# Keys and values of a narrow attention projected ahead, its maxima through single PSUM banks, and a first attention that holds V stationary

## The chip, the cores and the metric

The kernel runs on one NeuronCore of a Trainium2 chip. The metric is the device time of one execution in microseconds (us), lower is better. Nine executions of the kernel before had a median of 1678.9 us (1672.92 to 1681.6). Engines are called by their names: TensorE (PE in the profile), VectorE (DVE), ScalarE (ACT), GpSimd (POOL) and SyncE (SP), which issues most transfers.

## The reference

A network of twelve blocks, each added to a residual `x` of shape [4, 128, 128] (batch, token, channel); most read a layernorm of it. Four blocks attend to a context of shape [4, 2048, 96]. Two of these are changed here, and a feed-forward block lies between two changes.

The first block (`_L0_xattn_ref`, the kernel's `bit_attention`) uses linear layers with ternary weights and int8-rounded activations. Its attention runs twice, and its keys, which are also its values, are 64 wide and used twice over:

```python
for Wa, ba in ((W_att0, b_att0), (W_att1, b_att1)):
    kv = bitnet_linear(image_embeds, Wa, ba)
    k = jnp.concatenate([kv, kv], axis=-1)
    scores = jnp.einsum('bse,bpe->bsp', fused, k) * inv_sqrt_e
    attn = jax.nn.softmax(scores, axis=-1)
    fused = fused + 0.1 * jnp.einsum('bsp,bpe->bse', attn, k)
```

The tenth block (`_L3_xattn_ref`, `narrow_attention`) has eight heads of sixteen channels:

```python
q = x @ Wq + bq
k = y @ Wk + bk          # y: the context
v = y @ Wv + bv
# heads of 16
weight = softmax(einsum('bhqd,bhkd->bhqk', q, k) * scale)
out = einsum('bhqk,bhkd->bhqd', weight, v) ... @ Wo + bo
```

The ninth (`_L2_ffn_ref`, `bit_ffn`) is layernorm, a quantized linear layer to 512, Gelu, layernorm, and a quantized linear layer back to 128.

## The kernel before

`Net` holds one method per block; they are called in order, and each passes `nxt()` to load the next block's weights. A framework allots tiles from pools (a pool of `bufs=n` reuses n buffers per tag and makes the next user wait for the last reader), and the order of instructions on each engine is fixed when the kernel is built. PSUM has eight banks of 512 float32 per partition.

**`bit_attention`** (L812 on) works in eight units: two rounds (`att0`, `att1`) times four batches. A unit's 2048 context positions are sixteen chunks of 128, in two groups g of eight. `scores(g)` (L959) writes transposed scores, 128 positions by 128 queries per chunk, with keys of even chunks in partitions 0 to 63 and those of odd chunks in 64 to 127. `reduce_max` (L961), a transpose (L966), a second reduction (L968) and a spreading transpose (L971) give the maximum; `weights(g)` subtracts it (L977) and takes the exponential (L979) into `p`. `values` (L988) holds each chunk of `p` stationary and streams 65 columns of `v`, 64 values and a column of ones that gives the softmax sum; then a reciprocal (L992), a scaling (L994), a transpose (L996) and an addition (L997) into `fused`. The loop interleaves units: maximum of i, scores 0 of i+1, weights of i, values of i-1, scores 1 of i+1, queries of i+2. At i = 3 and 4 a context mask is loaded and converted on GpSimd (L1027).

**`bit_ffn`** (L1768 on) needs the mean of its weights' absolute values: a matmul `tot` (L1786), then `wm`, `wi` and, per half, `t` twice and `qw` (L1788 to L1797), all on VectorE. `q_tr` transposes the quantized input, `h_ps` (L1828) is the first product. The second layernorm writes a tile `hn`.

**`narrow_attention`** (L593 on) keeps heads in groups of four, g = 0 to 3, each in 32 partitions; s = 0, 1 picks the group of four. After the layernorm and `q_ps`, `project(0)` computes keys `k_ps` (L645) and values `v_ps` (L656) of batch 0; `maxima(0, 0)` streams the keys past each head's queries (`s_ps`, L673), reduces them (L678), transposes the maxima (`m_tr`, L684) and adds them into spare rows of `q` (L685), so that the later scores come out already reduced by them. The loop then runs over batches b and halves s; `weighted` makes four steps of four chunks each: transposed scores `t_ps` (L697), their exponential `p` (L703), and, one step late, the values `av` (L710), whose seventeenth row is the softmax sum. Beside each step run one quarter of the next half's maxima and, while s and b allow, one piece of `project(b + 1)`. `finish` (copies of `av`, `o_tr`, `on_tr`, `y`) closes a batch after the first step of the next. PSUM: three double banks shared by `q_ps`, `k_ps`, `v_ps`, `s_ps` and `t_ps`, one bank for all small transposes, one for `av`. Copies out of PSUM alternate between ScalarE (L323) and VectorE (L325).

Of the kernel before, what the change touches and what calls it, by code (L numbers as in the profile page):

```python
# [19 lines left out]
B = 4  # L20
# [250 lines left out]
class Net:  # L271
# [320 lines left out]

    def narrow_attention(self, nxt):  # L593
# [7 lines left out]
        wqo, wkv = self.load("qo3"), self.load("kv3")  # L601
        scale = 1.0 / math.sqrt(ND)
        with ExitStack() as es:
# [3 lines left out]
            ps = es.enter_context(tc.tile_pool(name="na_sc", bufs=3, space=PSUM))  # L607
            mi = es.enter_context(tc.tile_pool(name="na_mi", bufs=1, space=PSUM))
# [4 lines left out]
            tr = mi.tile([P, B, P], F32, tag="mi", name="tr_x")  # L613
# [24 lines left out]
            def project(b):  # L638

                kT = wk.tile([P, 2, S], F32, tag="kT", name="kT")  # L640
                v = wk.tile([P, NCH, NH * VW], F32, tag="v", name="v")
                for at in range(0, S, 512):
                    mm = ps.tile([P, 2, 512], F32, tag="sc", name="k_ps")
                    for s in range(2):
                        nc.tensor.matmul(  # L645
                            mm[:, s], wkv[:, s * P : s * P + P],
                            self.ctxT[: DC + 1, b * S + at : b * S + at + 512], start=True, stop=True)
                    self.copy(kT[:, :, at : at + 512], mm)
                    yield kT, v
                for c in range(0, NCH, 6):  # L650
                    mm = ps.tile([P, 2, 512], F32, tag="sc", name="v_ps")
                    n = min(6, NCH - c)
                    for j in range(n):
                        at = b * S + (c + j) * P
                        w = NH * VW
                        nc.tensor.matmul(  # L656
                            mm[:, j // 3, j % 3 * w : j % 3 * w + w], self.ctxT[: DC + 1, at : at + P],
                            wkv[:, 2 * P : 2 * P + w], start=True, stop=True)
                    for j in range(0, n, 3):
                        k = min(3, n - j)  # L660
                        self.copy(
                            v[:, c + j : c + j + k].rearrange("p c w -> p (c w)"), mm[:, j // 3, : k * w])
                    yield kT, v

            def maxima(b, s, kT):

                qs = q[:, s, b * T : b * T + T]
# [1302 lines left out]
```

## Time and profile before

| | us |
|---|---|
| median of nine executions | 1678.9 |
| the profiled execution, its own time | 1678.22 |
| its span in the trace | 1676.2 |
| mean granted TensorE clock | 0.812 |
| TensorE busy (share of the span) | 1251.0 (75%) |
| VectorE busy | 999.3 (60%) |
| ScalarE busy | 620.6 (37%) |
| GpSimd busy | 140.8 (8%) |
| `bit_attention`, loop over units | 80.5 to 187.3 |
| `bit_ffn`, from the end of alibi to its `x` | 1302.5 to 1359.9 |
| `narrow_attention`, `q_ps` to first `t_ps` | 1367.3 to 1395.7 |
| `narrow_attention`, loop | 1395.7 to 1607.7 |

A line of the groups reads: line, engine, operation, output <- inputs, shape, count | busy us, mean ns of one | idle time of the engine before it and what ended that. An fp32 matmul appears as two records. The granted clock is a share of full speed, 1.00 or 0.50 at any moment. Starts are us from the start of the span.

### The profile page before, as it was taken

How to read it: one execution, taken by the hardware profiler on the slowest of the kernel's cores; microseconds unless marked ns; L12 is line 12 of the kernel's file. 1: busy time of each engine (PE TensorE's matmuls, PEld its weight loads, DVE VectorE, ACT ScalarE, POOL GpSimd, SP SyncE). 2: the span in 40 equal slices, each digit the busy share in tenths (PEclk: the TensorE clock that was granted, in tenths of full speed). 3: DMA queues.
4: the chain of work that ended last, by engine and by line, in shares of the span. 5: the costliest groups of instructions: out<-in, count | busy, mean ns of one | idle time of the engine just before them, and what ended most of it. 6: DMA issues, size and time to landing. Idle time of an engine off the chain costs nothing.

```text
span 1676.2 us, 15539 instructions
## 1 busy us (share of the span) xinstructions
PE 1251.0 (75%) x6142; PEld 675.5 (40%) x6142; DVE 999.3 (60%) x1568; ACT 620.6 (37%) x796; POOL 140.8 (8%) x108
## 2 busy tenths in 40 slices
PE   2689547677899999999847054989958148989857
PEld 0378412223434444444313032654426034555544
DVE  8955468994256676767567954124657665354335
ACT  3722255552145555646433001324523102333332
POOL 0010004462000000000001000000020100000000
PEclk9965558798579999999968576978978567898778
DMA  5000000005000000000010004000000000000010
GB/s 156 1 1 1 0 0 1 25 0 142 17 26 1 0 1 1 0 0 1 1 50 1 0 0 125 1 23 19 1 2 1 9 0 1 2 2 1 6 48 7
DMA packets 9371, 28.19 MB, mean 17 GB/s; under 512 B 1175, under 2 KB 7104, under 8 KB 8142
## 3 DMA queue, kind: packets, MB, share of 16 engines
q1 hardware_dynamic: 8174, 24.88, 5.1%
q10 hardware_dynamic: 1120, 2.27, 0.4%
q8 instruction: 50, 0.82, 0.2%
q14 instruction: 27, 0.22, 0.0%
HBM read 26.88 MB, written 0.26 MB: 16 GB/s over the span
## 4 chain that ended last, share of the span: by engine, by line
PE 63%; DVE 24%; ACT 5%; issue 4%; POOL 3%; DMA 1%; POOLq 0%; ACTq 0%; DVEq 0%; SPq 0%
PE sc L495 12%; PE av L529 12%; PE s_ps L673 4%; DVE na_m L678 3%; PE av L988 3%; PE mm L1317 3%; PE t_ps L697 3%; PE q_ps L438 2%; DVE h L1234 2%; PE av L710 2%; PE h_ps L1666 2%; PE y_ps L1673 2%; PE st L959 2%; PE y_ps L1239 2%; POOL hc L1237 1%
## 5 line engine op out<-in xcount | busy, mean ns | idle before, releaser
L495 PE MATMUL sc<-q_aug,ctxT 99*128 99x512 f32 x448 | 213.2, 602 | 1.8 <-DVE q_aug L439 1.8
L529 PE MATMUL av<-s,ctx 128*97 128x512 f32 x448 | 206.8, 597 | 6.6 <-ACT s L527 6.0
L526 DVE TENSOR_TENSOR s<-s,mbs 128x1024 f32<-128x1024 f32 x112 | 132.3, 1217 | 38.8 <-ACT mbs L521 38.8
L497 ACT COPY s<-sc 128x1024 f32<-128x1024 f32 x112 | 112.9, 1008 | 114.8 <-PE sc L495 114.8
L678 DVE TENSOR_REDUCE na_m<-s_ps 128x2 f32<-128x1024 f32 x64 | 75.8, 1220 | 91.2 <-PE s_ps L673 91.0
L527 ACT ACTIVATE s<-s 128x1024 f32<-128x1024 f32 x112 | 115.5, 1056 | 35.9 <-DVE s L526 35.3
L505 DVE TENSOR_TENSOR m<-m,s 128x1024 f32<-128x1024 f32 x72 | 87.9, 1220 | 66.3 <-ACT s L497 66.3
L529 PEld LDWEIGHTS av<-s,ctx 128*97 128x97 f32 x448 | 73.1, 165 | 125.0 <-issue 105.5
L495 PEld LDWEIGHTS sc<-q_aug,ctxT 99*128 99x128 f32 x448 | 82.7, 193 | 93.9 <-issue 82.7
L1239 PE MATMUL y_ps<-hc,consts 128*128 128x512 f32 x128 | 75.2, 722 | 33.7 <-POOL hc L1237 30.8
L703 ACT ACTIVATE p<-t_ps 128x1024 f32<-128x1024 f32 x64 | 62.0, 1021 | 92.4 <-PE t_ps L697 92.4
L1237 POOL TENSOR_TENSOR hc<-h,cs 128x1024 f32<-128x1024 f32 x32 | 77.5, 2430 | 86.2 <-DVE h L1234 86.0
L1234 DVE TENSOR_TENSOR_SCAN h<-dA,dbu 128x512 f32<-128x512 f32 x64 | 74.4, 1202 | 3.7 <-ACT dA L1231 3.5
L673 PE MATMUL s_ps<-kT,q 32*128 32x512 f32 x256 | 66.1, 720 | 1.9 <-ACT p L703 1.0
L341 POOL TENSOR_TENSOR ln_sq<-ln_xc 128x512 f32<-128x512 f32 (+1 forms) x19 | 23.3, 1226 | 507.0 <-DVE ln_xc L339 500.5
L697 PE MATMUL t_ps<-q,kT 32*128 32x128 f32 x1024 | 56.3, 329 | 8.8 <-DVE na_m L678 5.8
L1239 PEld LDWEIGHTS y_ps<-hc,consts 128*128 128x128 f32 x128 | 26.0, 222 | 83.2 <-POOL hc L1237 57.0
L697 PEld LDWEIGHTS t_ps<-q,kT 32*128 32x128 f32 x1024 | 46.6, 223 | 27.1 <-DVE na_m L678 14.7
L1231 ACT ACTIVATE dA<-delta,A 128x508 f32<-128x508 f32 x64 | 42.7, 688 | 33.1 <-DVE h L1234 32.2
L358 PE MATMUL tr_xnT<-consts,xn 128*128 128x128 f32 x32 | 8.8, 429 | 60.1 <-DVE xn L348 41.3
L988 PEld LDWEIGHTS av<-kv,p 128*128 128x128 f32 x256 | 53.2, 319 | 0.2 <-issue 0.2
L988 PE MATMUL av<-kv,p 128*128 128x65 f32 x256 | 52.9, 399 | 0.0
(574 smaller groups left out, 2083.6 us busy)
## 6 DMA issues: line engine op xcount, KB each, us to landing
w_moe<-in_moe SPq DMA_DIRECT2D x2, 2048.0 KB, 8.0
ctxT<-in_ctxT SPq DMA_DIRECT2D x4, 768.0 KB, 12.6
rows<-in_rows ACTq DMA_DIRECT2D x1, 2048.0 KB, 12.0
w_l3f<-in_l3f SPq DMA_DIRECT2D x1, 1920.0 KB, 8.0
w_l0f<-in_l0f SPq DMA_DIRECT2D x1, 1024.0 KB, 4.9
w_mamba<-in_mamba SPq DMA_DIRECT2D x1, 976.0 KB, 18.9
w_r<-in_r SPq DMA_DIRECT2D x1, 960.0 KB
consts<-in_consts SPq DMA_DIRECT2D x1, 832.0 KB, 17.2
```

The source lines that it names most:

```text
L495: nc.tensor.matmul(sc[:, i], self.ctxT[:, at : at + P], u.q, start=True, stop=True)
L497: nc.scalar.copy(s, sc)
L526: nc.vector.tensor_sub(p, p, bc_mid(u.mb, 2))
L527: nc.scalar.activation(p, p, AF.Exp)
L529: nc.tensor.matmul(u.av[: DC + 1], self.ctx[:, u.b * NCH + chunks[2 * j + i]], p[:, i], start=j + i == 0, stop=j == n - 1 and i == 1)
L673: nc.tensor.matmul(ts[g // 2][:, g % 2], qs[lo : lo + 32], kT[lo : lo + 32, s, j * 512 : j * 512 + 512], start=True, stop=True)
L678: nc.vector.tensor_reduce(part[:, at : at + 2], t, axis=AX, op=ALU.max, negate=True)
L697: nc.tensor.matmul(ts[g // 2][:, g % 2, j], kT[g * 32 : g * 32 + 32, s, at : at + P], qs[g * 32 : g * 32 + 32], start=True, stop=True)
L988: nc.tensor.matmul(av[:, 0:65], u.ts[g][:, h * (HC // 2) + c], u.v[:, ch], start=g + h + c == 0, stop=g + h == 2 and c == HC // 2 - 1)
L1234: nc.vector.tensor_tensor_scan(h[:, half], self.flat(dA), dbu[:, half], 0.0, ALU.mult, ALU.add)
L1237: nc.gpsimd.tensor_mul(hc, h, bc_mid(cs, 2))
L1239: nc.tensor.matmul(y[:, half], self.ident, hc[:, half], start=n == 0, stop=n == 15)
```

## The change

Three things are changed.

`narrow_keys`, new, is called after `alibi_attention`, ahead of `bit_ffn`. It loads the weights `kv3` (before, they came with the block's other weights) and projects keys and values of batches 0 and 1 through three single PSUM banks, every copy on ScalarE. Batches 2 and 3 are projected inside the loop of `narrow_attention`, in the s = 0 steps of b = 1 and 2, four pieces a step; a piece is now one bank.

In `narrow_attention` the double banks go from three to two and serve `t_ps` and `q_ps` only. A ring `sp` of three single banks serves `s_ps`, all small transposes and the projections. `maxima` handles one head per tile and reduces it by itself (128x512, where it was 128x1024); two heads are issued ahead of `t_ps` and two ahead of `av` in each step. `weighted` yields twice a step, and `finish` comes after the values of the first step.

In `bit_attention` V is stationary (64 columns) and `p` streams (128 columns). Even chunks write the output's partitions 0 to 63, odd ones 64 to 127. The softmax sums come from three additions on GpSimd per group and two matmuls with a matrix of ones, which leave the sum in every partition; its reciprocal (128x128) and a multiplication scale the values, a matmul with `fold` adds both halves into both, and one VectorE operation adds the result into `fused`. The column of ones and the transpose are gone.

In `bit_ffn` the second layernorm works in place and one tile takes another's buffer.

```diff
--- before.py
+++ after.py
@@ -590,6 +590,44 @@
 
 
 
+    def narrow_keys(self, es):
+        pool = es.enter_context(self.tc.tile_pool(name="na_w", bufs=1))
+        self.wkv = pool.tile(list(self.A["kv3"].shape), F32, name="w_kv3")
+        self.nc.sync.dma_start(self.wkv, self.A["kv3"])
+        self.kvp = es.enter_context(self.tc.tile_pool(name="na_kv", bufs=2))
+        self.kv = {}
+        with self.tc.tile_pool(name="na_kvps", bufs=3, space=PSUM) as ps:
+            for b in range(2):
+                for self.kv[b] in self.project(ps, b, self.nc.scalar.copy):
+                    pass
+
+    def project(self, ps, b, copy):
+
+        nc, wkv = self.nc, self.wkv
+        kT = self.kvp.tile([P, 2, S], F32, tag="kT", name="kT")
+        v = self.kvp.tile([P, NCH, NH * VW], F32, tag="v", name="v")
+        for at in range(0, S, 512):
+            for s in range(2):
+                mm = ps.tile([P, 512], F32, tag="s", name="k_ps")
+                nc.tensor.matmul(
+                    mm, wkv[:, s * P : s * P + P], self.ctxT[: DC + 1, b * S + at : b * S + at + 512],
+                    start=True, stop=True)
+                copy(kT[:, s, at : at + 512], mm)
+                yield kT, v
+        w = NH * VW
+        for c in range(0, NCH, 3):
+            mm = ps.tile([P, 512], F32, tag="s", name="v_ps")
+            n = min(3, NCH - c)
+            for j in range(n):
+                at = b * S + (c + j) * P
+                nc.tensor.matmul(
+                    mm[:, j * w : j * w + w], self.ctxT[: DC + 1, at : at + P],
+                    wkv[:, 2 * P : 2 * P + w], start=True, stop=True)
+            copy(v[:, c : c + n].rearrange("p c w -> p (c w)"), mm[:, : n * w])
+            yield kT, v
+
     def narrow_attention(self, nxt):
 
 
@@ -598,19 +636,19 @@
 
 
         nc, tc = self.nc, self.tc
-        wqo, wkv = self.load("qo3"), self.load("kv3")
+        wqo = self.load("qo3")
         scale = 1.0 / math.sqrt(ND)
         with ExitStack() as es:
             one = es.enter_context(tc.tile_pool(name="na1", bufs=1))
             wk = es.enter_context(tc.tile_pool(name="na2", bufs=2))
             pp = es.enter_context(tc.tile_pool(name="na3", bufs=4))
-            ps = es.enter_context(tc.tile_pool(name="na_sc", bufs=3, space=PSUM))
-            mi = es.enter_context(tc.tile_pool(name="na_mi", bufs=1, space=PSUM))
+            ps = es.enter_context(tc.tile_pool(name="na_sc", bufs=2, space=PSUM))
+            sp = es.enter_context(tc.tile_pool(name="na_s", bufs=3, space=PSUM))
             avp = es.enter_context(tc.tile_pool(name="na_av", bufs=1, space=PSUM))
             xn = one.tile([P, B, C], F32, name="xn")
             self.layernorm(one, self.x, xn)
             nc.vector.tensor_add(self.x, self.x, bc_mid(self.row("bo3"), B))
-            tr = mi.tile([P, B, P], F32, tag="mi", name="tr_x")
+            tr = sp.tile([P, B, P], F32, tag="s", name="tr_x")
             for b in range(B):
                 nc.tensor.transpose(tr[:, b], xn[:, b], self.ident)
             xT = one.tile([P, N], F32, name="xT")
@@ -635,52 +673,23 @@
                 os.append(t)
             nxt()
 
-            def project(b):
...
             def maxima(b, s, kT):
 
                 qs = q[:, s, b * T : b * T + T]
                 part = self.small(16, "na_m")
                 for j in range(4):
-                    ts = [ps.tile([P, 2, 512], F32, tag="sc", name="s_ps") for _ in range(2)]
-                    for g in (0, 2, 1, 3):
-                        lo = g * 32
+                    for g in range(4):
+                        t = sp.tile([P, 512], F32, tag="s", name="s_ps")
+                        rows = slice(g * 32, g * 32 + 32)
                         nc.tensor.matmul(
-                            ts[g // 2][:, g % 2], qs[lo : lo + 32], kT[lo : lo + 32, s, j * 512 : j * 512 + 512],
-                            start=True, stop=True)
-                    for i, t in enumerate(ts):
-                        at = j * 4 + i * 2
-                        nc.vector.tensor_reduce(part[:, at : at + 2], t, axis=AX, op=ALU.max, negate=True)
-                    yield
+                            t, qs[rows], kT[rows, s, j * 512 : j * 512 + 512], start=True, stop=True)
+                        at = j * 4 + g
+                        nc.vector.tensor_reduce(part[:, at : at + 1], t, axis=AX, op=ALU.max, negate=True)
+                        yield
                 t = nmx[s]
                 nc.vector.tensor_reduce(
                     t[:, ND::32], part.rearrange("p (j g) -> p g j", g=4), axis=AX, op=ALU.min)
-                tr = mi.tile([P, B, P], F32, tag="mi", name="m_tr")
+                tr = sp.tile([P, B, P], F32, tag="s", name="m_tr")
...
+                    yield
                     while late:
                         late.pop()()
                     late.append(values)
@@ -720,7 +730,7 @@
...
-                tr = mi.tile([P, B, P], F32, tag="mi", name="o_tr")
+                tr = sp.tile([P, B, P], F32, tag="s", name="o_tr")
...
-                tr = mi.tile([P, B, P], F32, tag="mi", name="on_tr")
+                tr = sp.tile([P, B, P], F32, tag="s", name="on_tr")
...
-                y = mi.tile([P, B, P], F32, tag="mi", name="y")
+                y = sp.tile([P, B, P], F32, tag="s", name="y")
...
-            for kv in project(0):
-                pass
-            run(maxima(0, 0, kv[0]))
+            def take(g, n):
+
+                for _ in range(n):
+                    if g is not None:
+                        next(g, None)
+
+            kv = self.kv[0]
+            take(maxima(0, 0, kv[0]), 17)
             done = None
             for b in range(B):
                 av = avp.tile([P, 2, P], F32, tag="av", name="av")
-                more = iter(project(b + 1)) if b + 1 < B else iter(())
-                ahead = []
+                ahead = self.kv.get(b + 1)
+                more = iter(()) if ahead or b + 1 == B else iter(self.project(sp, b + 1, nc.scalar.copy))
                 for s in range(2):
                     if s == 0:
                         top = maxima(b, 1, kv[0])
                     else:
                         top = maxima(b + 1, 0, ahead[0]) if ahead else None
-                    for i, _ in enumerate(weighted(b, s, *kv, av)):
-                        if done and i == 0:
+                    steps = weighted(b, s, *kv, av)
+                    for i in range(NCH // 4):
+                        take(top, 2)
+                        next(steps)
+                        ahead = next(more, ahead)
+                        take(top, 2)
+                        next(steps)
+                        if done:
                             finish(*done)
                             done = None
-                        if top:
-                            next(top)
                         ahead = next(more, ahead)
-                    run(top)
+                        if s == 0:
+                            ahead = next(more, ahead)
+                            ahead = next(more, ahead)
+                    take(top, 1)
                 done = (b, av)
                 kv = ahead
             late.pop()()
@@ -812,7 +834,7 @@
             one = es.enter_context(tc.tile_pool(name="bit1", bufs=1))
             wk = es.enter_context(tc.tile_pool(name="bit2", bufs=2))
             big = es.enter_context(tc.tile_pool(name="bit_big", bufs=2))
-            BIG = NS // 2 + B * NCH * 65
+            BIG = NS
...
-                v = kv[:, NS // 2 :].rearrange("p (c w) -> p c w", w=65)
-                nc.gpsimd.memset(v[:, :, 64:65], 1.0)
+                v = kv[:, NS // 2 :].rearrange("p (c w) -> p c w", w=64)
...
-                        v[:, j * NCH : j * NCH + NCH, 0:64], mm.rearrange("p (c w) -> p c w", w=64))
+                        v[:, j * NCH : j * NCH + NCH], mm.rearrange("p (c w) -> p c w", w=64))
 
             class Unit:
 
@@ -949,6 +970,7 @@
...
                     u.mh = wk.tile([P, 2, P], F32, tag="mh", name="mh")
+                    u.total = wk.tile([P, 2, P], F32, tag="total", name="total")
 
...
+                    half = p[:, 0 : HC // 2]
+                    a = wk.tile([P, HC // 2, P], F32, tag="qtmp", name="psum")
+                    nc.gpsimd.tensor_add(a, half, p[:, HC // 2 :])
+                    nc.gpsimd.tensor_add(a[:, 0:2], a[:, 0:2], a[:, 2:4])
+                    nc.gpsimd.tensor_add(u.total[:, g], a[:, 0], a[:, 1])
+
                 def values(u):
+
                     av = ps.tile([P, 512], F32, tag="mm", name="av")
                     for g in range(2):
-                        for h in range(2):
-                            for c in range(HC // 2):
+                        for c in range(HC // 2):
+                            for h in range(2):
                                 ch = u.b * NCH + 2 * (g * (HC // 2) + c) + h
                                 nc.tensor.matmul(
-                                    av[:, 0:65], u.ts[g][:, h * (HC // 2) + c], u.v[:, ch],
-                                    start=g + h + c == 0, stop=g + h == 2 and c == HC // 2 - 1)
-                    r = self.small(1, "rsum")
-                    nc.vector.reciprocal(r, av[:, 64:65])
-                    o = wk.tile([P, 2, 64], F32, tag="o", name="o")
-                    nc.vector.tensor_scalar(o, bc_mid(av[:, 0:64], 2), r, u.osc10, ALU.mult, ALU.mult)
-                    mm = ps.tile([P, 512], F32, tag="mm", name="o_tr")
-                    nc.tensor.transpose(mm[:, 0:P], self.flat(o), self.ident)
-                    nc.vector.tensor_add(u.fb, u.fb, mm[:, 0:P])
+                                    av[h * 64 : h * 64 + 64, 0:T], u.v[:, ch], u.ts[g][:, h * (HC // 2) + c],
+                                    start=g + c == 0, stop=g == 1 and c == HC // 2 - 1)
+                    mm = ps.tile([P, 512], F32, tag="mm", name="rsum")
+                    for g in range(2):
+                        nc.tensor.matmul(mm[:, 0:T], self.ones, u.total[:, g], start=g == 0, stop=g == 1)
+                    o = wk.tile([P, T], F32, tag="o", name="o")
+                    nc.vector.reciprocal(o, mm[:, 0:T])
+                    nc.vector.tensor_mul(o, o, av[:, 0:T])
+                    nc.tensor.matmul(mm[:, T : 2 * T], self.flat(fold), o, start=True, stop=True)
+                    nc.vector.scalar_tensor_tensor(u.fb, mm[:, T : 2 * T], u.osc10, u.fb, ALU.mult, ALU.add)
 
...
-                t = one.tile([P, B, d], F32, tag=f"qt{j}", name="qt")
+                t = one.tile([P, B, d], F32, tag=("qt", "ln2_sq")[j], name="qt")
...
-            hn = one.tile([P, B, 512], F32, name="hn")
-            self.layernorm(one, h, hn, w=self.row("ln2_g"), b=self.row("ln2_b"), tag="ln2")
-            q, sc = quantized(hn, 512, 1)
+            self.layernorm(one, h, h, w=self.row("ln2_g"), b=self.row("ln2_b"), tag="ln2")
+            q, sc = quantized(h, 512, 1)
...
-    ("qk2", "vo2"), ("l2a",), ("l2f",), ("qo3", "kv3"), ("l3a",), ("l3f",),
+    ("qk2", "vo2"), ("l2a",), ("l2f",), ("qo3",), ("l3a",), ("l3f",),
 ]
...
+            if BLOCKS[i][0] == "alibi_attention":
+                nes = es.enter_context(ExitStack())
+                net.narrow_keys(nes)
+            if BLOCKS[i][0] == "narrow_attention":
+                nes.close()
```

More of the change, by code (lines that the diff above doesn't have):

```diff
@@ L636, in narrow_attention @@
             nxt()
-            def project(b):
[L640 to L663, printed above, removed]
             def maxima(b, s, kT):
```

## The prediction

> **What bounds the kernel now.** I read the page first, then busy time by stage, then the groups and the timeline inside the two attentions that change. Within 0.2%, 3.4 us, a measurement of this kernel can hardly tell a difference from no change.
>
> From the page, the busy shares in 40 slices of 41.9 us and the chain that ended last:
>
> ```profile
> PE   2689547677899999999847054989958148989857
> PEclk9965558798579999999968576978978567898778
> ...
> PE 63%; DVE 24%; ACT 5%; issue 4%; POOL 3%; DMA 1%; POOLq 0%; ACTq 0%; DVEq 0%; SPq 0%
> ```
>
> Slices 3 and 4 (the first attention) have TensorE 0.8 and 0.9 busy at half the clock; slices 33 to 37 (the narrow attention) 0.8 to 0.9 at 0.7 to 0.9 clock. Both stages are TensorE's. In slices 31 and 32, where `bit_ffn` runs, TensorE is nearly empty. Busy time by stage (us, then the five engines, the granted clock in the column before DMA share and GB/s):
>
> ```profile
> 102.90:187.30 84.40, 76.52 (x397) 69.90 (x397) 39.05 (x72) 14.27 (x18) 7.51 (x2) 0.50 0.00 1
> 1302.50:1359.90 57.40, 7.16 (x43) 4.56 (x42) 42.30 (x63) 5.37 (x6) 6.53 (x7) 0.51 0.02 6
> 1368.30:1382.30 14.00, 14.00 (x53) 7.99 (x51) 4.83 (x6) 3.02 (x4) 0.00 (x0) 0.85 0.00 1
> 1382.30:1395.70 13.40, 9.36 (x38) 2.80 (x37) 10.48 (x12) 1.78 (x2) 0.00 (x0) 0.77 0.00 0
> 1395.70:1450.90 55.20, 50.54 (x661) 30.85 (x662) 24.56 (x29) 20.38 (x24) 0.00 (x0) 0.90 0.01 1
> 1450.90:1464.60 13.70, 13.70 (x79) 5.83 (x77) 2.85 (x4) 4.09 (x6) 0.00 (x0) 0.50 0.00 1
> ```
>
> In order: the first attention's loop, bound by TensorE at clock 0.50; `bit_ffn`, bound by VectorE (42.3 of 57.4); the exposed projection of batch 0; the maxima of batch 0, first half, alternating TensorE and VectorE; the narrow loop's first batch; the step from batch 0 to 1, at half clock. The first attention's largest group, in its loop:
>
> ```profile
> L988 PE MATMUL av<-kv,p 128*128 128x65 f32 x224 | 48.8, 415 | 0.0
> L959 PE MATMUL st<-fq,kv 64*128 64x128 f32 x144 | 20.6, 446 | 4.3 <-DVE fq L948 2.7 <-DVE p L977 1.6
> ```
>
> Each matmul leaves two records. The values take over half of the stage. One projecting step of the narrow loop, from its timeline:
>
> ```profile
> 1414.82 1.98 PE L645 MATMUL k_ps<-ctxT,w_kv 97*128 97x512 f32 x4
> ...
> 1416.73 1.77 PE L697 MATMUL t_ps<-q,kT 32*128 32x128 f32 x32
> ...
> 1418.43 1.07 PE L710 MATMUL av<-p,v 128*17 128x128 f32 x32
> 1418.61 1.94 ACT L703 ACTIVATE p<-t_ps 128x1024 f32<-128x1024 f32 x2 [0.76 <-PE t_ps L697]
> ```
>
> A step is 5.93 us (`av` starts at 1412.51 and 1418.43). Without a projection (b=3, s=0) it is about 4.8, with neither projection nor maxima 2.3.
>
> **First attention.** The values now hold V stationary (64 columns) and stream p (128 columns), the two chunk halves in the two column halves. Cold, 16 matmuls took 6.97 us a unit. A pair of 64-row score matmuls, which also streams 128 columns through a half array twice, took 0.26 us a record, 0.52 a pair (16 records in 2.08 us at 125.93). By that row the eight pairs of values take 4.2 us. Added on TensorE: two ones-matmuls and the fold, 0.43 each cold, against one removed transpose. VectorE gains a reciprocal of 128x128 (the one of 128x64 took 0.55, that of 128x8 0.21: 0.94 by the slope), a multiply (0.28) and loses 0.17 and 0.41. GpSimd gains three adds per half: by the rows 1.04 (128x512), and less for 256 and 128, about 2.0, so 4.0 a unit, inside the period.
>
> Walking one unit in the new queue order (maximum's transpose, scores 0, spread, values, sums, scores 1, fold, next queries), cold: transpose 0.43, scores 2.08, spread 0.43, values 4.2, sums 0.86, scores 2.08 (10.1); then VectorE must reduce (1.22) and multiply (0.28) before the fold (0.45), queries (0.43) and the next transpose: 12.4 us. The period before was 13.7 (146.6 to 160.2). At the full clock TensorE's part shrinks to 5.7, and VectorE sets the period: two subtractions and two reductions 4.9, reciprocal 0.94, seven small ones 2.0, with the wait behind the scores 8.2. Which clock? The loop stays at 0.50 though TensorE's records cover 0.91 of it. The trace's clock changes at steps of 3.413 us. Adding up, in each such window, the records' streamed columns times the share of the array that they use, the value windows do 0.44 of what half a full-clock window of 128x128 matmuls gives, the score windows at most 0.59; at 474.7 us (0.66) and 1355.3 us (0.62) such a window was followed by full clock, at 1386.1 (0.54) by half. The new order has ten dense microseconds at up to 0.86, then 2.5 sparse ones, so I expect the clock to alternate: period 10.3, the mean of 12.4 and 8.2. Five full periods give 17, the two shorter ends 2, the last unit's tail 1.5 (values -3, reciprocal, multiply and fold +1.5). At units 3 and 4 the mask's two 3.76 us instructions stand in GpSimd's queue between the sums, and their transfer must wait for a buffer that the sums now share: cost 2, up to 5. **Sum -19**; all cold -9, all at full clock -33.
>
> The Trainium skill ("TensorE: Matmul & The Clock Gate", Part 1) says the array needs one busy window of about 3.4 us to go to the full clock. By the busy share alone this loop would be at full clock already, and the change would bring only the difference between two warm periods, a few us; the trace's 0.50 speaks against counting busy time.
>
> **Projection ahead.** After `alibi_attention` all of batches 0 and 1 is projected: 16 key matmuls of 0.86 (two records 0.43 apart) and 32 value matmuls of 0.26, 22 us, and 3 for the half clock at the start. The weights' DMA is moved from behind `w_qo` to SP's queue right after alibi and lands beside its last matmuls; the first key matmul still waits until alibi's last operation at 1303.2. ACT's 28 copies (0.5 each, 14 us) lie beside TensorE; `bit_ffn`'s own small ACT work waits at most about 0.4 twice. But the weights' mean `tot` (L1786, at 1303.3 before) is now behind all of these in TensorE's queue: 1328.6. What hangs on it, `wm`, `wi`, two `t`, `qw` (2.7) and `qT` (0.5), comes after the first layernorm and quantization, done at 1319.9, so `h_ps` starts near 1332 instead of 1321.1: **+11**. If it is all exposed, +25; if the scheduler's order on VectorE lets it go beside, +8.
>
> **Narrow start.** From `q_ps` to the first `t_ps` it was 28.4 us (1367.3 to 1395.7): projection 14, maxima 13.4. The projection leaves. The maxima's 16 tiles go through three single banks with 16 reductions of 128x512 (0.67 to 0.69, as 128x512 reductions at L343 and L335): 11 plus starts, and at the empty clock up to 14; with queries and transposes about 23 us. **-5.5** (0 to -9).
>
> **Narrow loop.** Step: `t_ps` 1.09, `av` 1.07, two pairs of `s_ps`. Four heads side by side took 1.14 to 1.38; two heads, at half clock at 1455.17, 2.08 for four records, hence 1.04: two pairs cost 2.1, so 0.9 a step is lost. Step 4.2, against VectorE's 4 x 0.68 = 2.7 and ACT's 1.94; the waits of 0.76 for `p` and for `na_m` that each step shows go, because scores and weights no longer share three double banks. Batches 2 and 3 are projected in the s=0 steps of b=1, 2: 3.1 a step and 0.4 for banks whose copies queue behind the exponentials. Steps before: 3 x (7 x 5.93 + 4.8) + 4 x 4.8 + 4 x 2.3 = 167. After: b=0 33.6, b=1 and 2 47.6 each, b=3 26: 155. The other 45 us of the loop's 212 are the steps between halves and batches, where TensorE waits for the reduction, `m_tr` and `q` (9.4 and 1.9 in all) and drops to half clock. Now a pair of scores stands ahead of that wait: 8 less. **Sum -20** (0 to -35).
>
> The Trainium skill ("TensorEngine Tiling (Array Packing)", Key Properties) says that changing the tiling mode drains TensorE; the new step changes mode twice fewer without a projection, twice more with one. The trace shows `s_ps` at 1464.69 right behind `av`; the sum takes nothing for it.
>
> Smaller edits: the layernorm in place, the shared tag and the smaller tile change no instruction's size; they add order only where VectorE runs in series anyway: 0.
>
> **Total**: -19 + 11 - 5.5 - 20 = -33.5 against the profiled 1678.2, which is 0.7 below the median of 1678.9: 1645.
>
> **Rivals.**
> 1. Slower, by the ring of three. If TensorE waits at each pair of scores for the reduction that frees a bank, every half step costs w more. There are 56 half steps with scores; -33.5 is used up at w = 0.6. Should it wait for a whole reduction, 0.69, the total is +5: 1684. For: projections and the small transposes draw on the same ring, behind ACT's exponentials. Against: VectorE needs 2.7 of 4.2 us.
> 2. Slower, values not side by side. 16 x 0.52 = 8.3 instead of 4.2 cold, eight units: +33 on the cold -9, so +24, total +9.5: 1688. It decides from 0.45 us a matmul. Against: 17-column `av` matmuls in four column groups took 1.07 us for 32 records of 128 columns, 0.033 each; alone, two transposes of 128 columns took 0.44 at half clock (`o_tr`, 1450.09), hence 0.11 a record at the full one.
> 3. The first attention turns to full clock throughout: -33 there, total -47.5: 1631. Against: the sparse 2.5 us of each unit.
> 4. Off the path: the loop stays as long (0) because steps between batches take the gain, the rest holds: -13.5, 1665.
>
> **How the numbers follow.** Forecast 0.50, rival 1 0.15, rival 2 0.08, rival 3 0.12, rival 4 0.15. Range: 3 and 4 lie within; downward, full clock and the loop's better bound together give 1616, taken at 1614; upward, 1 and 2: 1688. Faster 0.75: the forecast, 3 and 4 make 0.77, less 0.02 for terms that add up badly; with 0.01 of rival 1 that is 0.03 within 0.2%; slower 0.22.
>
> **What would show it.** Values' start to start period near 10 and clock above 0.5 in 103 to 187; a row of `av` in that stage with records near 0.26 (else rival 2); `tot` near 1328 and `h_ps` 11 later than before; 23 us from `q_ps` to `t_ps`; steps of 4.2 in b=0; waits of `s_ps` for `na_m` below 0.3 a pair (else rival 1). The forecast is wrong if the narrow loop does not shrink, or if its clock falls below the 0.9 of b=0 before.

## The result, and the profile after

The changed kernel took 1623.9 us (median of 10 runs, 1617.3 to 1634.6) against 1680.1 for the kernel before beside it: a ratio of 0.970, 95% interval 0.967 to 0.972. The forecast was 1645 in a range of 1614 to 1688, so the time lies inside it and the sign was right, but the gain was 56 us where 33.5 were summed. The spans of the two profiled executions, 1676.2 and 1623.1, give the difference stage by stage. The loop is taken here to its last addition into `x`, 1612.3 us before and 1560.5 after, and `bit_ffn` from the end of alibi's last addition, 1304.0 before and 1279.5 after.

| stage | before | after | difference | forecast |
|---|---|---|---|---|
| to the end of `bit_attention` | 202.9 | 178.5 | -24.4 | -19 |
| `bit_ffn`, from the end of alibi | 55.9 | 69.5 | +13.6 | +11 |
| narrow attention, `q_ps` to first `t_ps` | 28.4 | 23.1 | -5.3 | -5.5 |
| narrow attention, loop | 216.6 | 181.0 | -35.6 | -20 |
| all else | | | -1.4 | 0 |

The page of the changed kernel, the same lines as before:

```profile
PE   2567456676999999999847143889958726999957
PEclk9788568798589999999968676886989765899888
...
PE 63%; DVE 23%; ACT 6%; issue 4%; POOL 3%; DMA 1%; POOLq 0%; ACTq 0%; DVEq 0%; SPq 0%
```

In slices 3 and 4 TensorE fell from 0.8 and 0.9 busy to 0.6 and 0.7, and its clock rose from 0.6 and 0.5 to 0.8 in both. In slices 35 to 38, the narrow attention's, it is now 0.9 busy in each at a clock of 0.8 to 0.9. Of the two slices, counted from one, in which most of `bit_ffn` runs, 32 is now 0.7 busy with the projection (before 0.1), and 33 is still nearly empty at 0.2 (before 0.4). Busy time by stage, in the order first attention, `bit_ffn`, narrow start, batches 0 and 1 of the loop:

```profile
92.40:161.30 68.90, 51.61 (x507) 42.48 (x507) 53.48 (x85) 16.66 (x21) 43.31 (x47) 0.85 0.01 2
1279.50:1349.00 69.50, 30.27 (x138) 18.47 (x138) 41.23 (x60) 20.72 (x35) 6.53 (x7) 0.67 0.02 7
1356.40:1379.50 23.10, 20.39 (x39) 8.51 (x41) 12.11 (x20) 0.00 (x0) 0.00 (x0) 0.50 0.00 0
1379.50:1418.10 38.60, 36.78 (x548) 23.70 (x548) 21.55 (x36) 16.79 (x17) 0.00 (x0) 0.87 0.01 2
1418.10:1466.70 48.60, 46.83 (x633) 28.76 (x631) 23.19 (x41) 23.62 (x33) 0.00 (x0) 1.00 0.01 2
```

The clock in the first attention rose from 0.50 to 0.85. VectorE does about the same work in `bit_ffn` as before (41.2 us against 42.3 in a stretch that began 1.5 us earlier), but the stage is 13.6 us longer, so it waits. The whole of batch 1 ran at full clock, its beginning included, where the step from batch 0 to 1 stood at 0.50 before. The groups that answer to the first attention's two of before:

```profile
L1017 PE MATMUL av<-p,kv 128*64 128x128 f32 x256 | 19.9, 311 | 0.3 <-DVE fused L1027 0.3
L981 PE MATMUL st<-fq,kv 64*128 64x128 f32 x176 | 16.4, 340 | 2.1 <-DVE p L999 2.1
```

The values take 19.9 us for all eight units; before, seven took 48.8. The whole narrow loop, before and after:

```profile
1395.70:1612.30 216.60, 193.93 (x2443) 117.08 (x2443) 86.46 (x105) 77.61 (x92) 0.00 (x0) 0.85 0.01 2
1379.50:1560.50 181.00, 168.90 (x2395) 105.35 (x2393) 81.95 (x146) 82.44 (x106) 0.00 (x0) 0.93 0.01 2
```

The mean clock rose from 0.85 to 0.93. Counted from the single changes of the clock in the traces, 66.4 us of the loop ran at half clock before and 24.0 after. One step of the narrow loop, batch 0, from its timeline:

```profile
1405.07 0.70 PE L684 MATMUL s_ps<-kT,q 32*128 32x512 f32 x2
...
1405.24 0.50 PE L706 MATMUL t_ps<-q,kT 32*128 32x128 f32 x4
1405.60 0.59 PE L684 MATMUL s_ps<-kT,q 32*128 32x512 f32 x2
1406.03 0.95 PE L706 MATMUL t_ps<-q,kT 32*128 32x128 f32 x26
...
1407.21 1.94 ACT L712 ACTIVATE p<-t_ps 128x1024 f32<-128x1024 f32 x2 [2.02 <-PE t_ps L706]
...
1408.02 1.07 PE L719 MATMUL av<-p,v 128*17 128x128 f32 x32
...
1409.20 0.50 PE L706 MATMUL t_ps<-q,kT 32*128 32x128 f32 x4
```

The step is 3.96 us (1405.24 to 1409.20) where 4.2 was forecast. `t_ps` starts between the two records of a pair of `s_ps`: the four row groups serve two kinds of matmul at once, which the sum had put one behind the other.

### The profile page after: what moved, and what is told of

It reads as the page before. It is cut to its first block, busy times and chain, and to the rows that moved or that the text cites. A ratio compares the mean times of both kernels' runs of the same rounds, so it can differ in the third digit from the quotient of the medians.

```text
span 1623.1 us, 15762 instructions
## 1 busy us (share of the span) xinstructions
PE 1211.4 (75%) x6182; PEld 639.2 (39%) x6182; DVE 1000.1 (62%) x1612; ACT 634.9 (39%) x832; POOL 178.4 (11%) x154
## 4 chain that ended last, share of the span: by engine, by line
PE 63%; DVE 23%; ACT 6%; issue 4%; POOL 3%; DMA 1%; POOLq 0%; ACTq 0%; DVEq 0%; SPq 0%
PE sc L495 12%; PE av L529 12%; PE s_ps L684 4%; PE mm L1347 3%; PE q_ps L438 2%; DVE h L1264 2%; PE t_ps L706 2%; PE k_ps L614 2%; PE h_ps L1696 2%; PE y_ps L1703 2%; PE y_ps L1269 2%; PE av L719 1%; POOL hc L1267 1%; PE o_ps L1768 1%; POOL ln_sq L341 1%
## 5 line engine op out<-in xcount | busy, mean ns | idle before, releaser
L687 DVE TENSOR_REDUCE na_m<-s_ps 128x1 f32<-128x512 f32 x128 | 82.3, 686 | 77.1 <-PE s_ps L684 77.1
L684 PE MATMUL s_ps<-kT,q 32*128 32x512 f32 x256 | 88.0, 736 | 1.7 <-DVE na_m L687 1.7
L345 ACT ACTIVATE ln_sd<-ln_v,eps 128x4 f32<-128x4 f32 (+1 forms) x19 | 5.7, 300 | 111.7 <-DVE ln_v L343 111.7
## 6 DMA issues: line engine op xcount, KB each, us to landing
consts<-in_consts SPq DMA_DIRECT2D x1, 832.0 KB, 17.1
```

The costliest lines, as they stand in the source:

```text
L684: nc.tensor.matmul(t, qs[rows], kT[rows, s, j * 512 : j * 512 + 512], start=True, stop=True)
L687: nc.vector.tensor_reduce(part[:, at : at + 1], t, axis=AX, op=ALU.max, negate=True)
```

## The experiments

Each run's edit is against the changed kernel unless it says otherwise.

**The first attention alone** (the kernel before with the new `bit_attention`).

> The kernel before with the first attention's part of the change alone. Theory A (the three parts act in separate stages and simply add): the first block ends 24 us earlier as in the changed kernel (178.5 instead of 202.9 us) and the whole is 24 us faster, ratio 0.985 to 0.987. Theory B (part of the gain comes from elsewhere, such as a shifted clock window or the transfers): less than 18 or more than 30 us.

Measured: 1654.5 us; the medians differ by 21.2, the ratio is 0.989 (0.981 to 0.997; one run of the kernel before beside it was 19 us below its median, which widens the interval). The first block ended at 181.1 instead of 202.9, 21.8 earlier, and the span fell by 24.1. The other 2.3 us are not the block's but mostly the narrow loop's: in the code of the kernel before, it took 213.5 us with 59.9 of half clock instead of 216.6 with 66.5. Theory A, as far as this part goes: it acts in its own stage.

**Nothing projected ahead.**

```diff
-            for b in range(2):
-                for self.kv[b] in self.project(ps, b, self.nc.scalar.copy):
-                    pass
+            pass
...
-            kv = self.kv[0]
+            for kv in self.project(sp, 0, nc.scalar.copy):
+                pass
```

> The changed kernel, but nothing is projected ahead of bit_ffn: batch 0 is projected at the start of the narrow attention through the ring of single banks, batch 1 in the loop's b=0, s=0 steps. Theory A (the ring and the order of the step make the loop; the projections' place only moves work): bit_ffn 13 us shorter, start 14 longer, b=0 13 longer, 1637 us, and the loop stays at full clock nearly throughout. Theory B (it is the emptier loop that keeps the clock up): the half clock returns at each change of batch, loop above 205 us instead of 194, 1648 or more.

Measured: 1635.2 us. `bit_ffn` was back at 56.0, the start took 28.8 (5.7 more, not 14; part of the projection ran ahead of `q_ps`), the loop 195.0 with 31 us of half clock, and in it batch 0 took 56.6 for 38.6 (18 more, not 13). Theory A, for the total and the clock. Projecting ahead was worth 7.4 us by the spans (1630.5 against 1623.1): 20 saved in the narrow attention, 13.5 paid in `bit_ffn`. It is not what shortened the loop most.

**Scores behind instead of ahead.**

```diff
-                        take(top, 2)
                         next(steps)
+                        take(top, 2)
                         ahead = next(more, ahead)
-                        take(top, 2)
                         next(steps)
+                        take(top, 2)
```

> The changed kernel, with each pair of maxima scores issued behind the t_ps or av of its half step instead of ahead of them, so that nothing stands ahead of the wait for the maximum at a change of half. Theory A (the pair ahead covers that wait and keeps the clock up): 7 changes cost 2 to 4 us more each, with more half clock, 1638 to 1650 us. Theory B (the three single banks and the even step do it, wherever the pair stands): within 4 us of the changed kernel.

Measured: 1640.5 us, 16.5 more. The loop took 199.3 instead of 181.0, of it 45.7 at half clock instead of 24.0. The edit moves every pair, but the plain steps stay as they were (3.95 us in both); what is longer are the steps around a change of half or batch. The same matmuls in the same banks lose half the loop's gain when nothing stands ahead of the wait there: theory A.

**Projections behind `tot`, batch 1 behind `h_ps`** (`narrow_keys` then only loads the weights; `kps` is a pool of three single banks).

```diff
+            for self.kv[0] in self.project(kps, 0, nc.scalar.copy):
+                pass
             def quantized(x, d, j):
...
             nc.scalar.activation(self.flat(h), self.flat(h), AF.Gelu)
+            for self.kv[1] in self.project(ps, 1, nc.scalar.copy, "mm"):
+                pass
```

> The changed kernel, with the projection of batch 0 behind the weights' mean tot, and that of batch 1 behind h_ps, in two banks of bit_ffn's own. Theory A (bit_ffn lost 13.6 us because tot and what hangs on it stood behind all projections on TensorE): bit_ffn gets back 9 to 12 us, 1612 to 1615 us. Theory B (it lost them to ScalarE's copies and table loads beside its own operations): less than 4 us back.

Measured: 1628.5 us, no gain. `tot` ran at 1281.6, 0.7 us before the end of alibi's last addition as in the kernel before, and yet `bit_ffn` took 63.2. VectorE's longest wait in it (us in total, times, longest):

```profile
DVE ln_r L347 <- ACT ln_sd L345: 9.7, 3, 8.1
```

The root `ln_sd` of the first layernorm stands on ScalarE behind six copies of keys and a table load of 1.28 us, and the copies wait for TensorE, which waits 4.2 us for the weights. So both theories hold a part: 6.3 us of the 13.6 came back with `tot`, the copies held the rest. The loop, in the same code as in the changed kernel, took 187.7 with 44 us of half clock, and ate the 6.3.

**Both batches behind `h_ps`** (the pool of `h_ps` gets a third bank).

```diff
+            for b in range(2):
+                for self.kv[b] in self.project(ps, b, nc.scalar.copy, "mm"):
+                    pass
```

> The changed kernel, with both batches projected behind h_ps of bit_ffn, through three banks that h_ps itself uses, so that the transfer of the weights has long landed and no copy stands ahead of the first layernorm's root on ScalarE. Theory A (tot's place on TensorE and the root's place behind copies on ScalarE, both paced by the late weights, are all that bit_ffn lost): bit_ffn 56 to 59 us instead of 69.5; with the loop as in the changed kernel 1611 to 1613 us. Theory B (some other part of bit_ffn pays, now the second layernorm behind 14 copies): 64 us or more.

Measured: 1613.6 us, ratio 0.961 (0.958 to 0.964). `bit_ffn`, in one line of busy time by stage:

```profile
1278.80:1336.00 57.20, 31.36 (x136) 18.73 (x136) 40.77 (x60) 19.57 (x34) 6.54 (x7) 0.68 0.03 8
```

TensorE is busy for 31.4 us in it, where it was 7.2 before, and the stage is only 1.3 us longer than in the kernel before. Theory A.

**Column halves one after the other.**

```diff
-                        for c in range(HC // 2):
-                            for h in range(2):
+                        for h in range(2):
+                            for c in range(HC // 2):
```

> The changed kernel, with the values of the first attention in another order: four matmuls of one column half, then four of the other, instead of alternating. Theory A (the gain there is two column halves at work side by side): the 16 values matmuls of a unit take about twice as long, 3.9 us at full clock instead of 1.97, the clock stays at half for longer, and the first block ends 15 to 30 us later, 1640 to 1655 us. Theory B (it comes from shorter weight loads, 64 columns instead of 128, whatever the order): within 4 us of the changed kernel.

Measured: 1631.1 us, 7 more. From the first values to its end the block took 89.7 us; nine profiles with the changed kernel's first attention took 83.6 to 87.3 (86.2 in the changed kernel itself). A unit's values took 2.57 us at full clock instead of 1.97, not 3.9. Theory A has the direction and not the size. Before, the first unit's values took 4.12 us, 0.8 of it at half clock, so an estimated 3.7 at the full one. Of 1.7 us some 1.1 then come with the new shape whatever the order, and 0.6 with the halves side by side. The shape's weight loads are shorter at the same clock (medians of 137 ns against 192 at the full one, 230 against 333 at half); that they are the reason is not shown.

**All four heads in one go.**

```diff
-                        take(top, 2)
+                        take(top, 4)
                         next(steps)
                         ahead = next(more, ahead)
-                        take(top, 2)
                         next(steps)
```

> The changed kernel, with all four heads' scores of a step ahead of t_ps in one go instead of two and two. Theory A (three banks carry only two heads at a time; the fourth must wait for a reduction of 0.69 us): 0.7 to 1.4 us more for each of 28 steps, 1640 to 1660 us. Theory B (heads may run three or four side by side again and win back what a pair lost, 0.9 a step): 1605 to 1624 us.

Measured: 1658.7 us, 35 more; in the profiled execution, with 1671.3 the longest of four, the loop took 216.8 us, as long as before the change, 70 of them at half clock. TensorE's waits in it (us in total, times, longest) begin with

```profile
PE s_ps L684 <- DVE na_m L687: 13.1, 22, 0.8
```

In the changed kernel the same wait is 1.0 us in two places. The wait is 12 of the 36 us that the loop lost; half clock grew by 46 us. This is rival 1 made true: a ring of three fits two heads at a time.

**Idle matmuls in the first attention** (they stand ahead of the second scores and ahead of the fold; the reciprocal and what follows it are issued behind the second scores).

```diff
+                        nc.tensor.matmul(
+                            mm[:, 2 * T : 4 * T], self.ident, u.total[:], start=True, stop=True)
```

> The changed kernel, with up to four idle matmuls of 256 columns a unit (result unused) in the first attention, where TensorE waits for VectorE around the second scores. Theory A (half of the stage runs at half clock only because of these sparse stretches): granted clock above 0.9 between 90 and 160 us and the first block 5 to 8 us earlier. Theory B (the clock does not bind there any more, VectorE's queue does): no earlier, or up to 6 us later for the matmuls that stand in the way.

Measured: 1626.5 us. Busy time over four units, from values to values:

```profile
105.10:145.40 40.30, 31.90 (x333) 25.38 (x332) 32.70 (x53) 9.53 (x12) 27.08 (x26) 1.00 0.01 2
```

The clock was full, and the period still 10.1 us (40.3 by four), against 9.9 in the changed kernel (103.2 to 142.9), where the clock was 0.84. Theory A's gain did not come. But that the clock no longer binds here, theory B, is not shown either: the idle matmuls put the second scores 0.9 us later (3.40 us behind the start of the values at 126.10; 2.54 at 133.80 in the changed kernel), and the reciprocal now runs behind the second reduction instead of ahead of it, so the edit may have spent what the clock gave.

**Less work for VectorE, and for GpSimd.**

```diff
-                    nc.vector.reciprocal(o, mm[:, 0:T])
+                    nc.scalar.copy(o, mm[:, 0:T])
```

> The changed kernel without the reciprocal of the softmax sums in the first attention (ScalarE copies the sums instead, so the values are scaled by the sums themselves): VectorE loses 0.95 us a unit, the chain to the fold gains a copy of 0.27. Theory A (VectorE sets the unit's period of 9.3 us at either clock, being 0.87 busy there): the first block ends 5 to 7 us earlier. Theory B (TensorE's waits and half clock set it): less than 2 us earlier.

```diff
-                    nc.gpsimd.tensor_add(a, half, p[:, HC // 2 :])
-                    nc.gpsimd.tensor_add(a[:, 0:2], a[:, 0:2], a[:, 2:4])
-                    nc.gpsimd.tensor_add(u.total[:, g], a[:, 0], a[:, 1])
...
-                        nc.tensor.matmul(mm[:, 0:T], self.ones, u.total[:, g], start=g == 0, stop=g == 1)
+                        nc.tensor.matmul(mm[:, 0:T], self.ones, u.ts[g][:, 0], start=g == 0, stop=g == 1)
```

> The changed kernel without GpSimd's additions in the first attention (the matmuls with ones sum one chunk of p in each group in place of the eight chunks' total). Theory A (VectorE's operations with both operands in SBUF, the maximum of mh and the bias into fused, take 0.46 and 0.54 us on average instead of 0.28 because GpSimd works beside them): both go back to 0.28 and the first block ends 3 to 5 us earlier. Theory B (they are long for another reason, GpSimd costs nothing): both stay above 0.4, less than 1.5 us.

Measured: 1629.8 and 1628.2 us; the first block took 90.5 and 94.4 us from the first values, longer than with the work in place (83.6 to 87.3). Without the reciprocal VectorE waited 6.7 us for ScalarE's copies; without the additions it waited 8.4 for the matmuls of the sums, which now read `p` itself and hold its buffers. Both edits put a new wait in the place of the work, so these runs don't say whether VectorE's work is the bound. One part is settled, theory A on the two operations. Without GpSimd's additions the bias into `fused` (L970) is back at 0.28 us each time. So is the maximum of `mh` in seven of eight units:

```profile
L985 DVE TENSOR_TENSOR mh<-mh 128x128 f32<-128x128 f32 x8 | 5.6, 698 | 0.1
```

The mean of 0.70 comes from the eighth, 3.58 us beside the conversion of the mask that GpSimd still does. In the changed kernel such an operation ends 0.15 us behind the GpSimd operation beside which it began:

```profile
120.93 1.27 POOL L1006 TENSOR_TENSOR psum<-p 128x512 f32<-128x512 f32 x1
...
121.94 0.41 DVE L970 SCALAR_TENSOR_TENSOR fused<-cols,fused 128x128 f32<-128x128 f32 x1
```

Over the changed kernel's eight units the two operations took 3.4 us more than 0.28 each.

**Four heads at the start, on top of the late projections** (`maxima4` is `maxima` as the kernel before had it; the second run has no edit beyond late_ahead).

```diff
-            take(maxima(0, 0, kv[0]), 17)
+            take(maxima4(0, 0, kv[0]), 5)
```

> Both batches projected behind h_ps as in the run late_ahead, and the maxima of batch 0's first half in the form of the kernel before, four heads side by side in the two double banks that t_ps doesn't need yet, with reductions of 128x1024. Theory A (at the half clock of the start TensorE binds, four heads cost little more than two): from q_ps to the first t_ps 19 us instead of 23.2, and the loop starts at full clock sooner: 1605 to 1610 us. Theory B (the reductions bind, and the clock at the start is not moved): within 2 us of late_ahead.

> The kernel of late_ahead once more, beside late_warm on the same chip. By its first run 1613 us; its loop's half clock 15 to 45 us long, and the loop 175 to 188 us with it, since the changed kernel's identical loop took 175.0 us with 14.6 us of half clock, 181.0 with 24 and 187.7 with 44. If the loop's length doesn't go with its half clock, the clock is not what varies.

Measured: 1610.0 us (ratio 0.957, 0.952 to 0.961) beside 1613.9 (0.963, 0.960 to 0.966). The start took 20.8 instead of 23.1, 2.3 of the 4 expected; the loops 176.5 and 179.7 with 19.5 and 26.1 us of half clock. Both beat the changed kernel; late_warm is the fastest median of all, though its interval touches that of the other.

The following runs have the same code from the first `t_ps` on:

| run | half clock in the loop, us | loop, us |
|---|---|---|
| halves_apart | 14.6 | 175.0 |
| bit_fill | 14.7 | 175.1 |
| no_recip | 14.7 | 175.1 |
| late_warm | 19.5 | 176.5 |
| late_ahead | 23.9 | 180.9 |
| changed kernel | 24.0 | 181.0 |
| no_pool_sums | 24.0 | 181.0 |
| late_ahead2 | 26.1 | 179.7 |
| split_ahead | 44.3 | 187.7 |

The length goes with the half clock, 12.7 us over 29.7, or 0.43 us each. Single steps agree: the second step of batch 1, from `t_ps` to `t_ps`, took 14.07 us at full clock (halves_apart), 15.76 with 3.4 us of half clock (late_ahead2) and 17.32 with 6.8 (split_ahead).

## Why the prediction was right, point by point

**The sign and its order.** All four terms had the right sign. The narrow start was right to 0.2 us, and in part by luck: its maxima took 17.1 us (1361.27 to 1378.34) where 11 to 14 were forecast, at 2.85 us for every three heads, whose scores began only behind the first reduction of the three before; and queries and transposes took 6.1 where the sum leaves some 9. The loop passed the end of its own range (0 to -35) by a little. No rival came: waits of `s_ps` for `na_m` were 1.0 us in all, so the ring of three, rival 1, did not decide, and four_burst shows that it would have. Rival 2 supposed 8.3 us a unit at half clock for values not side by side, 0.52 a matmul by the row of the score matmuls; halves_apart's units took 2.57 at full clock and at most 4.4 with 3.9 of half clock, 0.16 to 0.28 a matmul. Its price was wrong, and with it the 24 us that it was to cost.

**The narrow loop, -35.6 instead of -20**, is the term that was mis-sized. By batch it went 53.3 to 38.6, 56.9 to 48.6, 58.3 to 50.3 and 48.1 to 43.5. Batch 0 was forecast at -12.7 and gave -14.7. Batches 1 and 2 were forecast at +1.3 each, with some 8 for all changes of half or batch, and gave -8.3 and -8.0. The step of the sum that failed is "8 less". With the steps as measured (3.95 us, 7.18 with a projection, and 3.26 with neither projection nor maxima, where `t_ps` waits for `p`; the sum had 4.2, 7.7 and 2.3) the steps come to 149.5 for the 155 of the sum. What is left of the loop, the changes of half and batch, fell from 49 to 31.5, about 18 less. The smaller steps, where `t_ps` runs beside `s_ps`, are the other 5 us of the miss.

A pair of scores ahead of the wait was priced as covered waiting. It also keeps the clock up. Half clock in the loop fell by 42.4 us; at 0.43 each they are worth an estimated 18, half of the gain. (The 0.43 is from the new loop; the two profiles of the old one, 216.6 and 213.5 us, give 0.47.) scores_behind, without the pair, gives back 18.3 us with 21.7 more of half clock, so some 9 of it are clock and the rest is waiting; no_ahead gives back 14.0 with 7.2 more, for batch 1's projection.

Part of the -35.6 is luck. The same code took 175.0 to 187.7 us in other kernels, and against the 216.6 before that would have been -42 to -29. One of the prediction's signs of being wrong is met as it is worded: batch 0 ran at 0.87, below the 0.9 of before. Its first steps hold 10.4 us of half clock, before 10.8, in a shorter batch; the whole loop rose to 0.93.

**`bit_ffn`, +13.6 instead of +11.** `tot` ran at 1308.1, 28.6 us after the end of alibi, where the sum had 24.6. The missing piece is the transfer of the weights, which was to land beside alibi's last matmuls:

```profile
1275.32 0.28 SPq L598 DMA_DIRECT2D w_kv<-in_kv  x1
...
1283.72 6.82 PE L614 MATMUL k_ps<-ctxT,w_kv 97*128 97x512 f32 x11 [5.72 <-DMA w_kv<-in_kv]
...
1290.33 0.30 ACT L345 ACTIVATE ln_sd<-ln_v,eps 128x4 f32<-128x4 f32 x1
...
1290.66 0.18 DVE L347 RECIPROCAL ln_r<-ln_sd 128x4 f32<-128x4 f32 x1 [7.65 <-ACT ln_sd L345]
...
1308.12 0.38 PE L1816 MATMUL tot<-bf_s,ones 128*128 128x2 f32 x2 [0.53 <-ACT v L628]
```

It took 8.4 us from issue, and TensorE waited 5.7 for it. The fourth line is a second miss: the root, behind three copies and a table load of 1.28 us, held VectorE for 7.65 us, not 0.4. It cost nothing here only because `tot` came later still; the input was quantized at 1300.8. split_ahead laid it bare.

**The first attention, -24.4 instead of -19.** The clock alternated as forecast (31 us of half clock from 85 to 165, before 69). Five full periods gave 21.6 us for the 17 of the sum, the ends and the tail 3.5 as forecast, and the mask, put at +2, cost nothing that shows: its two conversions run in periods of 9.3 and 9.1. The mean period came out at 9.9 for the forecast 10.3. The forecast let half of the time be at half clock; it was 12.5 of 39.7 us, and the sum's own 8.2 at full clock and 12.4 at half, mixed by that share, give 9.5. No run shows either of the two periods alone, for bit_fill's full clock comes with idle matmuls in the way. So the account fits, but what sets the unit's period, the clock or the chain of second scores, reduction, multiply, fold and maximum, stays open.

**Clock and column tiles.** The Trainium skill ("TensorE: Matmul & The Clock Gate", Part 1) lets one busy window of about 3.4 us bring the full clock. The trace differs if busy is read as time: in the narrow start TensorE's records cover 20.39 of 23.1 us, at 0.50 throughout. (The window shares of 0.44 to 0.66 in the prediction are too low for what they are called. Counted against a window filled with the 0.43 us records of 512 columns, the value windows do 0.25, the others of the loop up to 0.36, and those at 474.7 and 1386.1 do 0.40 and 0.32; as shares of half such a window these are twice as large. The order that the argument rests on stays, but it is no clean rule: the window at 1396.3 did 0.37 and was followed by half clock, the one at 1461.2 did 0.36 and was followed by full. The prediction's count of changes of the tiling mode is off too: by the order in the traces a step without a projection has two before and after, one with a projection four before and five after.) The Trainium skill ("TensorEngine Tiling (Array Packing)", Performance Considerations) offers the swap of stationary and streamed operand with two column tiles where the streamed side is narrow; the trace agrees that it pays, 1.97 us at full clock for an estimated 3.7 (at half clock 3.68 in bit_only for 6.93), but only 0.6 of the 1.7 is the two tiles at work side by side.

## What to carry to other kernels

Give TensorE something that doesn't depend on the wait ahead of every wait that recurs: here a pair of independent matmuls ahead of the waits at seven changes of half or batch is worth 18 us in all, by estimate half of it through the clock. When work is moved into an idle engine's time, look at every in-order queue that it is put into, that of the copies too, and put it behind the last short operation that somebody waits for: the same projections cost 13.6 us ahead of `bit_ffn`'s small matmul and root, and 1.3 behind them. Two versions of a stage are compared by its half clock as well as by its length, since the same code took 175 to 188 us.

## What the runs showed of the hardware that was not expected

Matmuls of 32 rows overlap also when they stream different lengths: `t_ps` (128 columns) started between the records of a pair of `s_ps` (512), and a step is shorter than the sum of its forecast parts, 3.96 us for 1.09, 1.07 and 2.1.

The granted clock changes only on a grid of 3.413 us in each trace, and the half clock of a stage goes with the place on that grid where it starts. The identical loop started 2.1 to 2.2 us behind a grid point in halves_apart, bit_fill and no_recip and had 14.6 or 14.7 us of half clock in all three; within 0.1 us of one in the changed kernel, no_pool_sums and late_ahead, with 23.9 or 24.0; and 0.45 us behind one in split_ahead, with 44.3. Some of these kernels differ only hundreds of microseconds earlier.

A VectorE operation of 128x128 with both operands in SBUF took 0.28 us alone. One that began beside a GpSimd operation and was held ended 0.15 us behind it, whatever its length: up to 1.24 us beside the additions in the changed kernel (L970, 0.54 on average), 3.58 beside the conversion of the mask (no_pool_sums).
